# A conv-attention hybrid on one core: order of score copies, moved squares and the k projection in layer 1

## The chip, the core and the metric

The kernel runs on one core of a Trainium2 chip. The metric is the device time of one execution in microseconds (us); the time before is the median of three runs. Layer 1 of each of the eight images is the stage that the change touches. All arithmetic is fp32.

## What is computed

The input is x of shape (8, 256, 32, 32): eight images, each seen as 1024 tokens of 256 channels.

Layer 0 projects tokens to q, k and v for 8 heads of width 64, softens the scores over the *query* axis, applies them to v, projects with w_out and adds the input. Layer 1 is:

```python
t = _to_tokens(x)
t = t + _L1_attn_ref(_ln_t(t), L1_attn_W)
t = t + _L1_ffn_ref(_ln_t(t), router_w, w1, b1, w2, b2)
# _L1_attn_ref(n, W):
xa = einsum('bnd,ed->bne', n, W)
scores = einsum('bne,bme->bnm', xa, n)
y = einsum('bnm,bmd->bnd', softmax(scores, axis=-1), n)
```

So layer 1's attention has one head of width 256 whose keys and values are both the normed tokens n. The last line is a mixture of eight experts of which each token uses two.

## The kernel before, in words

**Stages.** Images are taken one after another. For image b, `layer0` runs the eight heads in pairs; then `attend` runs layer 1's attention; then `normed` and `logits` prepare the routing. For the first seven images the expert work is put off: rows are sent out in the next image's layer 0, and one routed pass (`experts`) handles them after the last image's layer 0. The last image uses `dense`. While layer 1 of image b runs, three kinds of work of image b+1 that do not depend on it are offered as filler by class `Begin`: its projection to q (t = 0), its projection to k (t = 1), each four matmuls of 128x512 in two accumulations (`project`, L349) with two evictions by ScalarE (L336), and its values (`values`, L408), two matmuls for each block of 128 tokens and an add by VectorE (L416). `Begin.at(place)` is called at "norm 1", "normed 1", "last weights", "last products", "norm 2" and "normed 2"; each call makes one block of values, and "norm 1" makes q and "norm 2" makes k. The remaining two blocks come from `rest` in the next layer 0.

**attend.** `layer_norm` makes n1, `to_channels` turns it (nT), and WT times nT gives px for two halves of the channels (L700). One level of a seven-product (Strassen-Winograd) scheme computes the scores: the 1024x1024 score matrix is seen as 2x2 halves. xa is kept as a11, a12, a22, s3_ and the mixes t1_ to t4_, s1_, s2_, s4_ (L689 to L716). ScalarE copies a22 and then a12 out of PSUM (L712, L713); VectorE then makes s1_ from a22 (L714), s2_ (L715) and s4_ (L716).

Rows are handled in four pairs, `Pair(k)` for k = 0 to 3: block k of the upper half and block k of the lower half, 128 rows each. The constructor makes five of the seven products (L750): a11·b11 into x, which ScalarE copies to the left half of the even block's buffer (L738, called `one_` before and `self.first` after); a12·b21 into v; s2_·t2_ on top of x, copied to the right half (L742, `self.second`); s1_·t1_ into z; s3_·t3_ on top of x, copied to the odd block's right half (L745). VectorE adds v and z to two of the halves and keeps their minima (L760). `rest` adds the last two products (s4_·b22 into z, a22·t4_ on top of x). It then takes the maxima and softens: the even block by L760 and one activation over 1024 (L781); the odd block by L784 and two activations of 512, one out of PSUM (L788) and one in SBUF (L796). x and v are the two banks of one tile of a pool of three ("big"), which px, the projections, the transposes and the values also use. z is in a pool of two that the mixings use too.

**Turning.** The mixing y = P·n needs the softened block with keys on partitions. For the first and the last block of BLOCKS, `turn_now` transposes by TensorE (L832) and VectorE copies the result out (L834). For the six blocks between, `turn` lets VectorE transpose squares of 32x32 in place (L814) and then moves sixteen strips of squares, 32x256 each: eight by ScalarE copies, eight by DMAs of SyncE (both recorded as L825). `issue_after(ins)` around a move makes it follow `ins` on the engine of `ins`; on other engines it adds nothing.

**Mixing.** `mix(at, ...)` does eight matmuls of 128x256 (L842; in the trace sixteen records) and divides by the sum and adds the residual (L851). The order in the code is: pairs 0 and 1, rest of 0, the second block turned, rest of 1, the third block turned, `turn_now(0)`, pair 2, the fourth block turned, mixings 0 to 2, and so on; `mix(7)` is last.

**What sets the order.** [...] In the trace this is not the order of the code: where an instruction that is traced earlier is not expected to be ready, one traced later is put before it. So the k projection, traced after the last mixing, runs between mixings. After the last mixing VectorE takes statistics (L256, L257), ScalarE the square root (L260), VectorE scales (L261, L263), TensorE transposes n2 (L281) and VectorE copies it (L282); then come the logits (L895) and the next image's first scores (L489).

Of the kernel before, what the change touches and what calls it, by code (L numbers as in the profile page):

```python
# [12 lines left out]
AF = mybir.ActivationFunctionType  # L13
ALU = mybir.AluOpType
# [5 lines left out]
def kernel(  # L20
# [23 lines left out]
    nc = tc.nc  # L44
# [18 lines left out]
    NQ = P // SQ  # L63
# [25 lines left out]
    def big(name):  # L89

        return ps_big.tile([P, 1024], F32, tag="big", name=name)
# [6 lines left out]
    scrap = const.tile([P, 512], F32, name="scrap")  # L98
# [231 lines left out]
    evicted = {}  # L330
# [54 lines left out]
    class Begin:  # L385
# [35 lines left out]

        def at(self, place):

            if place == "norm 1" or place == "norm 2":
                self.project(True)
            self.values(1)

        def all(self):
# [241 lines left out]
    def attend(b, t1, fill, tick=nothing):  # L670
# [13 lines left out]
        HALF = S // 2  # L684
# [8 lines left out]
        a11, s3_, a12, a22 = (xa[:, e, n, :] for e in range(2) for n in range(2))  # L693
        s1_, s2_, s4_ = (mixes[:, 4 + i, :] for i in range(3))
        pxs = []
        for ec in range(NCC):
            px = big(f"px_{b}_{ec}")
            for dc in range(NCC):
                for n in range(NH2):
                    nc.tensor.matmul(  # L700
                        px[:, ts(n, 512)],
                        WT[:, dc, ts(ec, P)],
                        nT[:, dc, ts(n, 512)],
                        start=(dc == 0),
                        stop=(dc == NCC - 1),
                    )
            pxs.append(px)
            if ec == 0:
                nc.scalar.copy(a11, px[:, :HALF])
                tick(("xa", ec), nc.vector.tensor_sub(s3_, a11, px[:, HALF:]))  # L710
            else:
                nc.scalar.copy(a22, px[:, HALF:])  # L712
                nc.scalar.copy(a12, px[:, :HALF])  # L713
                nc.vector.tensor_add(s1_, a22, pxs[0][:, HALF:])  # L714
                nc.vector.tensor_sub(s2_, s1_, a11)  # L715
                tick(("xa", ec), nc.vector.tensor_sub(s4_, a12, s2_))  # L716
# [5 lines left out]
        class Pair:  # L722

            def __init__(self, k):
                self.k = k
                both = big(f"ps1_{b}_{k}")
                self.x, v = both[:, :HALF], both[:, HALF:]
                self.z = acc(f"ps1z_{b}_{k}")
                self.ex = [homes[EX[2 * k + h]] for h in range(2)]
                self.low = [  # L730
                    small.tile([P, 1], F32, tag=f"nlow{h}", name=f"nlow_{b}_{k}_{h}")
                    for h in range(2)
                ]
                left, right = (self.ex[0][:, ts(n, HALF)] for n in range(2))
                far = self.ex[1][:, ts(1, HALF)]
                at = ts(k, P)
                self.product(self.x, a11, b11, True)
                one_ = nc.scalar.copy(left, self.x)  # L738
                second = self.product(v, a12, b21, True)
                tc.declare_no_dep(second.ins, one_.ins, reason="the other bank")  # L740
                self.product(self.x, s2_, t2_, False)
                self.second = nc.scalar.copy(right, self.x)  # L742
                self.product(self.z, s1_, t1_, True)
                self.product(self.x, s3_, t3_, False)
                nc.scalar.copy(far, self.x)  # L745
                self.add(left, v, 3.0e38, self.low[0])
                self.add(far, self.z, 3.0e38, self.low[1])
# [23 lines left out]
            def rest(self):  # L771
                k = self.k
                self.product(self.z, s4_, b22, False)
                self.product(self.x, a22, t4_, False)
                nmax, ssum = [], []
                for h in range(2):
                    nmax.append(small.tile([P, 1], F32, tag="nmax", name=f"nmax_{b}_{2 * k + h}"))
                    ssum.append(small.tile([P, 2], F32, tag="ssum", name=f"ssum_{b}_{2 * k + h}"))
                ex0, ex1 = self.ex
                tick(("max", 2 * k), self.add(ex0[:, HALF:], self.z, self.low[0], nmax[0]))  # L780
                nc.scalar.activation(  # L781
                    ex0, ex0, AF.Exp, bias=nmax[0], scale=-1.0, accum_out=ssum[0][:, 0:1]
                )
                last = nc.vector.tensor_scalar(  # L784
                    scrap, self.x, -1.0, self.low[1], ALU.mult, ALU.min, accum_out=nmax[1]
                )
                tick(("max", 2 * k + 1), last)
                nc.scalar.activation(  # L788
                    ex1[:, :HALF],
                    self.x,  # L790
                    AF.Exp,
                    bias=nmax[1],
                    scale=1.0,
                    accum_out=ssum[1][:, 0:1],
                )
                nc.scalar.activation(  # L796
                    ex1[:, HALF:],
                    ex1[:, HALF:],
                    AF.Exp,
                    bias=nmax[1],  # L800
                    scale=-1.0,
                    accum_out=ssum[1][:, 1:2],
                )
                return [(2 * k, ex0, ssum[0][:, 0:1], None), (2 * k + 1, ex1, *self.halves(ssum[1]))]

            def halves(self, ssum):
                return ssum[:, 0:1], ssum[:, 1:2]

        def turn(i, ex, behind):


            at_sq, at_aT = SQ_AT[i]
            sq = homes[at_sq]
            nc.vector.transpose(sq, ex)  # L814
            if at_aT is None:
                aT = two.tile([P, S], F32, tag="tr", name=f"aT_{b}_{i}")
            else:
                aT = homes[at_aT]
            to = aT.rearrange("p (m a q) -> p a m q", a=NQ, q=SQ)
            since = sq.rearrange("p (m k q) -> p k m q", k=NQ, q=SQ)  # L820
            for a in range(NQ):
                for k in range(NQ):
                    move = nc.sync.dma_start if (a + k) % 2 else nc.scalar.copy
                    with tc.issue_after(behind.ins) if behind else nullcontext():
                        move(to[ts(k, SQ), a], since[ts(a, SQ), k])  # L825
            return [aT[:, ts(m, P)] for m in range(NT)]

# [9 lines left out]
        def mix(at, aT, ssum, more):  # L837
            i = BLOCKS[at]
            ahead = fill("last products") if at == NT - 1 else None
            py = acc(f"py_{b}_{i}")  # L840
            for m in range(NT):
                nc.tensor.matmul(  # L842
                    py[:, :D], aT[m], n1[:, m, :], start=(m == 0), stop=(m == NT - 1)
                )
            rs = small.tile([P, 1], F32, tag="rs1", name=f"rs1_{b}_{i}")
            if more is not None:
                nc.vector.tensor_add(rs, ssum, more)
                ssum = rs
            nc.vector.reciprocal(rs, ssum)
            with tc.issue_after(ahead.ins) if ahead else nullcontext():  # L850
                mixed = nc.vector.scalar_tensor_tensor(  # L851
                    t2[:, i, :], py[:, :D], rs, t1[:, i, :], ALU.mult, ALU.add
                )
            tick(("mixed", at), mixed)
# [3 lines left out]
        def turned(at, ex, ssum, more, behind=None):  # L858
            return at, turn(at, ex, behind), ssum, more

        pairs = [Pair(0), Pair(1)]
        first, second = pairs[0].rest()
        second = turned(*second)
        third, fourth = pairs[1].rest()
        third = turned(*third)
        now = turn_now(0, first[1])
        pairs.append(Pair(2))
        fourth = turned(*fourth, pairs[2].second)
        mix(0, now, *first[2:])
        mix(*second)  # L870
        fifth, sixth = pairs[2].rest()
        fifth = turned(*fifth)
        mix(*third)
        pairs.append(Pair(3))
        sixth = turned(*sixth, pairs[3].second)
        mix(*fourth)
        seventh, eighth = pairs[3].rest()
        seventh = turned(*seventh)
# [432 lines left out]
    class Results:  # L1311
# [96 lines left out]
        def tick(self, place, behind=None):  # L1408
            added, sent, stored = self.PLACES.get(place, (0, 0, 0))
            if place == ("max", 0):  # L1410
                self.scored = behind
            if added:
                with tc.issue_after(behind.ins):
                    for _ in range(added):
                        self.add()
            for _ in range(sent):
                self.gather(behind)
            for _ in range(stored):
                if self.whole:
                    b, total, n = self.whole.pop(0)  # L1420
                    store(b, total, n)
# [135 lines left out]
    for b in range(B):  # L1557
# [16 lines left out]
        norm = None  # L1574
# [54 lines left out]
```

## Time and profile before

| what | value |
|---|---|
| median of 3 runs | 2346.41 us (2345.22 to 2347.16) |
| the profiled execution, own time | 2352.09 us |
| its span, first to last instruction | 2350.1 us |
| granted TensorE clock, mean | 0.992 |
| TensorE busy | 2270.4 us, 97% of the span |
| VectorE, ScalarE, GpSimd busy | 1560.2, 1165.0, 412.1 us |
| moves of squares by ScalarE (L825), three groups | 102.9 + 25.7 + 25.6 us for 384 copies |
| one image's TensorE work in layer 1, 902.8 to 994.2 us | 89.33 us busy of 91.40 |
| start to start from one image to the next, images 1 to 5 | 242.8 us |

In a timeline each row gives the start and the duration in us, the engine, the line, the operation with output and inputs, and how many instructions were merged. The bracket has the idle time of the engine just ahead of the row, and the instruction that ended it. "SPq" is SyncE's queue of DMA issues; its durations are those of issuing, not of the data. A busy TensorE can be one whose matmul ends are modelled.

### The profile page before, as it was taken

Reading aid. Unit: us, or ns where it says so; the run is one execution under the profiler, and the core shown is the slowest. Engines: PE = TensorE matmul, PEld = TensorE weight load, DVE = VectorE, ACT = ScalarE, POOL = GpSimd, SP = SyncE. Lnnn points to the kernel's source line nnn. Section 1 sums busy time; section 2 is a strip of 40 time slices with the busy share of each in tenths; the row PEclk is TensorE's granted clock in tenths of the full one; section 3 lists DMA queues with packets and bytes.
Section 4 is the critical chain, followed back from the end, with each engine's and each line's share of the span. In section 5 each row is a group of like instructions: output and inputs, shape, how many; then the busy total and the mean of one; then the engine's idle time right before and its main releaser. Section 6 shows DMA issues by size and latency. Waiting matters only on the chain.

```text
span 2350.1 us, 37998 instructions
## 1 busy us (share of the span) xinstructions
PE 2270.4 (97%) x13059; PEld 1213.5 (52%) x13059; DVE 1560.2 (66%) x4029; ACT 1165.0 (50%) x2139; POOL 412.1 (18%) x392
## 2 busy tenths in 40 slices
PE   9999999999999999999999999999999899999798
PEld 3345534553456335633564355435553278885465
DVE  5775578557865786578647775677568856435765
ACT  3664466446635663656464646465546522224321
POOL 0000012000200030003000200020002125444663
PEclk9999999999999999999999999999999999999899
DMA  8995201020103010201020101100110237665664
GB/s 295 385 386 141 68 15 42 7 57 10 46 1 57 12 51 1 45 19 50 5 46 19 46 10 27 37 23 15 21 43 19 71 99 196 182 188 152 189 196 136
DMA packets 278760, 200.10 MB, mean 85 GB/s; under 512 B 189576, under 2 KB 232232, under 8 KB 276776
## 3 DMA queue, kind: packets, MB, share of 16 engines
q1 hardware_dynamic: 252472, 139.14, 21.0%
q0 software_dynamic: 25008, 58.01, 7.7%
q8 instruction: 104, 1.70, 0.3%
q10 hardware_dynamic: 1088, 0.52, 0.1%
q14 instruction: 88, 0.72, 0.1%
HBM read 108.88 MB, written 110.90 MB: 94 GB/s over the span
## 4 chain that ended last, share of the span: by engine, by line
PE 82%; ACT 5%; DVE 5%; DMA 4%; issue 3%; SPq 0%; POOL 0%; DVEq 0%; ACTq 0%; POOLq 0%
PE po L566 18%; PE psc L489 18%; PE py L842 7%; PE pqk L371 7%; PE pr L663 5%; PE ps L750 4%; PE pv L408 4%; PE ph L1246 3%; PE pe L1272 3%; PE pdh L1495 2%; PE px L700 2%; PE pdy L1519 2%; PE pqk L349 2%; PE ps1z L750 1%; DMA y<-yb 1%
## 5 line engine op out<-in xcount | busy, mean ns | idle before, releaser
L530 ACT ACTIVATE ex<-psc,nmax 128x1024 f32<-128x1024 f32 x512 | 570.5, 1115 | 308.8 <-DVE scrap L513 225.3
L489 PE MATMUL psc<-qk,qk 64*64 64x512 f32 x4096 | 580.3, 593 | 3.6 <-ACT ex L530 3.5
L566 PE MATMUL po<-ex,vs 64*64 64x512 f32 x4096 | 570.9, 593 | 10.3 <-SPq L576 9.4
L513 DVE TENSOR_SCALAR_CACHE_REDUCE scrap<-psc,nmax 128x512 f32<-128x512 f32 x512 | 384.4, 751 | 165.6 <-PE psc L489 137.9
L504 DVE TENSOR_REDUCE nmax<-psc 128x1 f32<-128x512 f32 x512 | 350.6, 685 | 10.8 <-PE psc L489 10.8
L489 PEld LDWEIGHTS psc<-qk,qk 64*64 64x64 f32 x4096 | 180.6, 132 | 282.2 <-ACT ex L530 130.2
L566 PEld LDWEIGHTS po<-ex,vs 64*64 64x64 f32 x4096 | 175.0, 132 | 285.3 <-issue 83.9
L1060 POOL DMA_INDIRECT rows<-n,d_at x112 | 109.2, 975 | 656.8 <-DVE nmax L504 656.5
L987 POOL TENSOR_TENSOR t<-t,n 128x2048 f32<-128x2048 f32 x8 | 36.2, 4524 | 900.9 <-DVE n L263 744.2
L371 PE MATMUL pqk<-xT,wqkv 128*128 128x512 f32 x384 | 171.2, 599 | 0.1
L336 ACT ACTIVATE qk<-pqk,b_qks 128x512 f32<-128x512 f32 x124 | 85.6, 690 | 122.3 <-PE pqk L371 77.2
L408 PE MATMUL pv<-wqkv,xT 128*128 128x512 f32 x256 | 123.5, 604 | 1.5 <-DVE v L416 1.0
L842 PE MATMUL py<-n,spare 128*128 128x256 f32 x512 | 117.3, 383 | 5.8 <-DMA out_dram<-oT 3.8
L1368 POOL DMA_INDIRECT yk<-y,yat x112 | 112.0, 1000 | 61.6 <-issue 24.7
L371 PEld LDWEIGHTS pqk<-xT,wqkv 128*128 128x128 f32 x384 | 71.0, 190 | 100.0 <-issue 76.5
L842 PEld LDWEIGHTS py<-n,spare 128*128 128x128 f32 x512 | 98.2, 192 | 32.7 <-issue 20.0
L663 PE MATMUL pr<-wo,res 128*128 128x256 f32 x512 | 111.9, 379 | 0.0
L663 PEld LDWEIGHTS pr<-wo,res 128*128 128x128 f32 x512 | 97.2, 190 | 17.0 <-ACT res L585 3.2
L825 ACT COPY spare<-home 32x256 f32<-32x256 f32 x256 | 102.9, 402 | 3.2
L1256 ACT ACTIVATE hb<-ph,wb 128x256 f32<-128x256 f32 x96 | 40.4, 471 | 125.7 <-issue 86.6
L530 ACT ACTIVATION_READ_ACCUMULATOR ex<-psc,nmax 128x1 f32 x512 | 99.0, 193 | 0.0
L1246 PE MATMUL ph<-xb,wb 128*128 128x256 f32 x384 | 91.8, 381 | 6.3 <-DMA wb<-wpack,w_at 4.7
(256 smaller groups left out, 2895.9 us busy)
## 6 DMA issues: line engine op xcount, KB each, us to landing
rows<-wb SPq DMA_DIRECT2D x7, 8192.0 KB
xr<-rows SPq DMA_DIRECT2D x252, 64.0 KB
y<-yb POOLq DMA_DIRECT2D x63, 256.0 KB
xs<-in_x_dram SPq DMA_DIRECT2D x64, 128.0 KB
spare<-home SPq DMA_DIRECT2D x256, 32.0 KB
out_dram<-oT SPq DMA_DIRECT2D x60, 128.0 KB
xT<-in_x_dram SPq DMA_DIRECT2D x7, 1024.0 KB
sums<-t SPq DMA_DIRECT2D x7, 1024.0 KB
```

The source lines that it names most:

```text
L371: mm = nc.tensor.matmul(pq[:, ts(n, 512)], wqkv[:, cc, t, ts(g, P)], xT[:, cc, ts(n, 512)], start=(cc == 0), stop=(cc == NCC - 1),)
L408: nc.tensor.matmul(pv, self.xT[:, cc, ts(i, P)], wqkv[:, cc, 2, :], start=(cc == 0), stop=(cc == NCC - 1),)
L489: mm = nc.tensor.matmul(pss[at, h][ts(c, DK), ts(n, 512)], k[r, j * P + c * DK : j * P + (c + 1) * DK], q[r, ts(n, 512)], start=True, stop ...
L504: firsts[at, h] = nc.vector.tensor_reduce(nmax, pss[at, h][:, ts(0, 512)], AX.X, ALU.max, negate=True)
L513: seconds[h] = nc.vector.tensor_scalar(scrap, pss[at, h][:, ts(1, 512)], -1.0, nmaxes[at, h], ALU.mult, ALU.min, accum_out=nmax,)
L530: nc.scalar.activation(ex, pss.pop((at, h)), AF.Exp, bias=nmaxes.pop((at, h)), scale=1.0, accum_out=sums[at][:, h : h + 1],)
L566: mm = nc.tensor.matmul(po[n][ts(h, DK), :], vss[at][keys, h, :], exps[at, h][keys, ts(n, 512)], start=(j == 0 and turn == 0), stop=(j == ...
L663: nc.tensor.matmul(pr[:, :C], res[:, g, ts(i, P)], wo[:, g, :], start=(g == 0), stop=(g == NPAIR - 1))
L750: return nc.tensor.matmul(to, stationary[:, ts(self.k, P)], moving, start=start, stop=True, skip_group_check=not start,)
L842: nc.tensor.matmul(py[:, :D], aT[m], n1[:, m, :], start=(m == 0), stop=(m == NT - 1))
L1246: last = nc.tensor.matmul(ph[:, ts(fc, BR)], wb[:, dc * FF + fc * P : dc * FF + (fc + 1) * P], xb[:, dc, :], start=(dc == 0), stop=(dc == ...
L1368: ins = nc.gpsimd.indirect_dma_start(out=self.slot(at)[:, k, :], out_offset=None, in_=self.group.y[:, :], in_offset=bass.IndirectOffsetOnAxis(
```

## The change

Four edits, all in layer 1's attention or in its fillers:

1. a12 is copied ahead of a22.
2. In pair 1 the odd block is softened ahead of the even one, so that the activation which reads the pair's PSUM comes first. Other pairs keep the order.
3. `turn` takes a pair of instructions to stay behind: the first for strips a = 0 and 1, the second for a = 2 and 3. The third block's turn moves in the code behind `turn_now(0)` and `Pair(2)`; its ScalarE moves are held behind pair 2's first copy (L738) for half of the strips and its second (L742) for the others. The fourth and sixth blocks stay behind the second copy of the next pair, as before.
4. The k projection ("norm 2") is issued on TensorE behind the last matmul of the last mixing.

```diff
@@ Begin.at
-            if place == "norm 1" or place == "norm 2":
+            if place == "norm 1":
                 self.project(True)
+            elif place == "norm 2":
+                with tc.issue_after(evicted["mixed"].ins):
+                    self.project(True)
             self.values(1)
@@ attend
             else:
+                nc.scalar.copy(a12, px[:, :HALF])
                 nc.scalar.copy(a22, px[:, HALF:])
-                nc.scalar.copy(a12, px[:, :HALF])
@@ Pair.__init__
-                one_ = nc.scalar.copy(left, self.x)
+                self.first = nc.scalar.copy(left, self.x)
                 second = self.product(v, a12, b21, True)
-                tc.declare_no_dep(second.ins, one_.ins, reason="the other bank")
+                tc.declare_no_dep(second.ins, self.first.ins, reason="the other bank")
@@ Pair.rest
+                def even():
+                    tick(("max", 2 * k), self.add(ex0[:, HALF:], self.z, self.low[0], nmax[0]))
...
+                def odd():
+                    last = nc.vector.tensor_scalar(
+                        scrap, self.x, -1.0, self.low[1], ALU.mult, ALU.min, accum_out=nmax[1]
+                    )
...
+                for half in (odd, even) if k == 1 else (even, odd):
+                    half()
@@ turn
-        def turn(i, ex, behind):
+        def turn(i, ex, behind=None):
...
-                    with tc.issue_after(behind.ins) if behind else nullcontext():
+                    with tc.issue_after(behind[a * 2 // NQ].ins) if behind else nullcontext():
                         move(to[ts(k, SQ), a], since[ts(a, SQ), k])
@@ mix
-                nc.tensor.matmul(
+                evicted["mixed"] = nc.tensor.matmul(
                     py[:, :D], aT[m], n1[:, m, :], start=(m == 0), stop=(m == NT - 1)
                 )
@@ attend, the order
         third, fourth = pairs[1].rest()
-        third = turned(*third)
         now = turn_now(0, first[1])
         pairs.append(Pair(2))
-        fourth = turned(*fourth, pairs[2].second)
+        third = turned(*third, (pairs[2].first, pairs[2].second))
+        fourth = turned(*fourth, (pairs[2].second, pairs[2].second))
         mix(0, now, *first[2:])
...
-        sixth = turned(*sixth, pairs[3].second)
+        sixth = turned(*sixth, (pairs[3].second, pairs[3].second))
```

More of the change, by code (lines that the diff above doesn't have):

```diff
@@ L779, in rest @@
                 ex0, ex1 = self.ex
[L780 to L803, printed above, removed]
+                def even():
+                    tick(("max", 2 * k), self.add(ex0[:, HALF:], self.z, self.low[0], nmax[0]))
+                    nc.scalar.activation(
+                        ex0, ex0, AF.Exp, bias=nmax[0], scale=-1.0, accum_out=ssum[0][:, 0:1]
+                    )
+                def odd():
+                    last = nc.vector.tensor_scalar(
+                        scrap, self.x, -1.0, self.low[1], ALU.mult, ALU.min, accum_out=nmax[1]
+                    )
+                    tick(("max", 2 * k + 1), last)
+                    nc.scalar.activation(
+                        ex1[:, :HALF],
+                        self.x,
+                        AF.Exp,
+                        bias=nmax[1],
+                        scale=1.0,
+                        accum_out=ssum[1][:, 0:1],
+                    )
+                    nc.scalar.activation(
+                        ex1[:, HALF:],
+                        ex1[:, HALF:],
+                        AF.Exp,
+                        bias=nmax[1],
+                        scale=-1.0,
+                        accum_out=ssum[1][:, 1:2],
+                    )
+                for half in (odd, even) if k == 1 else (even, odd):
+                    half()
                 return [(2 * k, ex0, ssum[0][:, 0:1], None), (2 * k + 1, ex1, *self.halves(ssum[1]))]
```

## The prediction, made before the change was run

> **What bounds the kernel now.** I read the page first, then the timeline of TensorE, ScalarE and SyncE over one image's layer 1. Part 1 of the page says that TensorE is the bound:
>
> ```profile
> PE 2270.4 (97%) x13059; PEld 1213.5 (52%) x13059; DVE 1560.2 (66%) x4029; ACT 1165.0 (50%) x2139; POOL 412.1 (18%) x392
> ```
>
> A change of order leaves TensorE's work as it is, so it can only win the stalls between matmuls. Image 3 stands for images 1 to 6, which repeat to about 0.1 us (the stage's TensorE busy time is 89.2 to 89.4 us in each). TensorE's timeline there (start, duration, instruction, and in brackets the idle time and who ended it):
>
> ```profile
> 930.64 1.02 PE L750 MATMUL ps<-nT,xa 128*128 128x512 f32 x2
> 931.96 1.12 PE L750 MATMUL ps<-nT,xa 128*128 128x512 f32 x2 [0.30 <-ACT xa L713]
> ...
> 945.13 1.88 PE L750 MATMUL ps<-nT,xa 128*128 128x512 f32 x4
> 947.25 1.98 PE L750 MATMUL ps<-nT,xa 128*128 128x512 f32 x4 [0.25 <-ACT home L788]
> 949.12 3.72 PE L842 MATMUL py<-n,aT 128*128 128x256 f32 x16
> 952.68 1.02 PE L408 MATMUL pv<-wqkv,xT 128*128 128x512 f32 x2
> 955.06 1.98 PE L750 MATMUL ps<-mixes 128*128 128x512 f32 x4 [1.36 <-ACT home L738]
> ...
> 981.10 3.62 PE L842 MATMUL py<-n,spare 128*128 128x256 f32 x16
> 984.55 2.74 PE L349 MATMUL pqk<-xT,wqkv 128*128 128x512 f32 x6
> 987.12 3.62 PE L842 MATMUL py<-n,spare 128*128 128x256 f32 x16
> 990.58 3.62 PE L842 MATMUL py<-n,aT 128*128 128x256 f32 x16
> 994.03 1.88 PE L408 MATMUL pv<-wqkv,xT 128*128 128x512 f32 x4
> 997.25 0.44 PE L281 MATMUL pt_n<-ident,n 128*128 128x128 f32 x2 [1.34 <-DVE n L263]
> ```
>
> Back to back, two records of a 512-wide product start 0.86 us apart (940.82 and 942.54 hold four, 1.72), so the true stalls, start against expected start, are a little longer than the brackets: 931.96 - 931.50 = 0.46; 947.25 - 946.85 = 0.40; 955.06 - 953.54 = 1.52; 997.25 - 995.75 = 1.50, and 0.29 more ahead of the logits at 1001.16. Sum **4.2 us an image**. The causes are in ScalarE's timeline:
>
> ```profile
> 946.43 0.67 ACT L788 ACTIVATE home<-ps,nmax 128x512 f32<-128x512 f32 x1
> 947.10 3.28 ACT L825 COPY aT<-home 32x256 f32<-32x256 f32 x8
> 950.39 0.72 ACT L796 ACTIVATE home<-home,nmax 128x512 f32<-128x512 f32 x1
> 951.11 3.28 ACT L825 COPY spare<-home 32x256 f32<-32x256 f32 x8
> 954.42 1.07 ACT L738 COPY home<-ps 128x512 f32<-128x512 f32 x2
> ```
>
> Pair 2's first score copy (L738) had its product ready near 946 and runs at 954.42, behind sixteen moves of squares. The other half of the moves goes through SyncE, which issues one after another at 0.65 us:
>
> ```profile
> 952.05 10.44 SPq L825 DMA_DIRECT2D spare<-home  x16
> 965.67 5.96 SPq L825 DMA_DIRECT2D home<-home  x8
> 971.74 10.44 SPq L825 DMA_DIRECT2D spare<-home  x16
> ```
>
> The last eight of these are the seventh turn's. They are issued by 982.18, and its mixing starts at 987.12 after the six k-projection records at 984.55.
>
> [...] this trace's chain of waits has the same for a SyncE move, 2.00 us at 227.65 in image 0, which I use. [...] the trace has 1283 ns at L260[...].
>
> **The change, part by part (one of images 1 to 6).**
>
> *a12 copied before a22.* The second product needs a12 only, so its 0.46 us wait goes. But a22 is then 0.48 later (931.32 for 930.84), so L714, which makes s1_, starts at 931.95 and ends at 932.64, and the next product, free at 932.36, waits some 0.35 for it. Gain 0.1 (0 to 0.46).
>
> *Odd half of pair 1 softened first.* Same three activations and two maxima, other order. L788, which frees the pair's two PSUM banks, goes from 946.43 to about 945.30; pair 3's products no longer wait: 0.40. Next late would be the first mixing at 949.12, which waits for the copy of pa (L834, 947.88 to 949.07) behind two transposes of 1.25; the copy is now traced ahead of the second of these, so it can run near 946.7. The third block's exponential ends at about 947.9 instead of 946.4; SyncE is busy with the second block's moves until 951.88, which hides it. Gain 0.4 (0 to 0.6).
>
> *Moves of the third block held.* Nothing is added: sixteen moves stay, eight by ScalarE at 0.41, eight DMAs by SyncE; the hold orders only ScalarE's, as the instruction waited for is ScalarE's. ScalarE needs from 945.30 2.5 us for pair 1 and 3.3 for the second block's moves, so L738 can run at 951.15 instead of 954.42. TensorE's first mixing ends at 952.1 to 952.6: the 1.52 us wait is gone. What is queued behind: four moves of the third block wait for L738, four for L742 (a product of 0.9 later), then the fourth block's eight, to about 959.5 if nothing stalls. The third mixing needs the DMAs, issued by 957.1, landed at 959.1; it would start near 959.8, so they are covered by 0.7. Pair 3's first copy, which today runs beside pair 2's, now loses to all these moves: near 959.5 in a gap, or behind pair 2's exponentials and the fifth block's moves near 966.3. In the second case TensorE lacks work ahead of the fourth mixing (landed at 964.5, free near 963.3: 1.2) and around the seventh. I take 0.9 given back of 1.5: gain 0.6 (-2.0 to 1.5).
>
> *k projection behind the last mixing.* Eight records, 3.44 us, and two evictions at 0.69 move behind 993.9. There VectorE's chain from the last mixing to pt_n takes 3.1 us; the projection covers all of it, and the values' add of 0.69 that today sits ahead of the reciprocal (995.95) can go. So the 1.79 us of the tail is covered. The loss is in front: the six records at 984.55 bridged the seventh turn's transfers. Those land at 982.18 + 2.0 = 984.2; without the 0.86 of projection at 980.24 the sixth mixing ends at 983.7: 0.5 bare, and where the remaining pv products fill it, they are missing in the tail. The evictions' readers, the next image's scores, come 6 us later: hidden. 0.7 is given back: gain 1.1 (-1.0 to 1.8, the low end being the third rival).
>
> Sum per image: 0.1 + 0.4 + 0.6 + 1.1 = **2.2**; images 1 to 6: **13.2**. Image 0 has the same stalls but waits of its own for transfers (1.3 more at 225.82): **1.6**. Image 7 has no projection to move; its stall at 2169.06 is 2.22, but its sixth and seventh mixings wait 3.79 and 1.98 for moves that SyncE issues between loads and stores held by VectorE, and those need not come sooner: **0.5** (-3 to 3). In all 15.3 us. The profiled execution took 2352.1 (span 2350.1), so it would take 2336.8; the median of runs is 2346.4, which gives **2331**.
>
> **Rivals.** *The last pair comes late* (slower). Pair 3's copies wait in ScalarE's queue; if its exponentials come later, the seventh turn's DMAs do, and nothing is left to bridge. Start of the seventh mixing plus 6.9 for two mixings plus 6.7 for the tail's chain against today's 1001.16 gives break-even at 987.55, moves landed 3.4 us later than today's 984.2. If the copies fall behind one more block of moves (3.3) and a product with its wait (1.3), it is 4.6: 1.2 lost an image, 8.4 in seven, **2355**. For it: pair 3 is traced last. Against: today there are 19 us from its first copy to its exponential (974.32), while pair 2 needs 8.7.
>
> *The fillers are spent early* (no change). With the projection barred, the pv products fill the waits ahead of the sixth and seventh mixings, and the tail is again bound by its chain, bare for 1.4 of today's 1.8; with the held moves' gain given back whole, 0.5 an image remains: **2343**.
>
> *The eviction gets ahead of the square root* (half the gain). The first k eviction is ready about 1.9 us after the last mixing, the root (L260) about 1.8. In the wrong order the root waits 0.69, and the table load, today done early at 988.03, may fall between: 1.28 more. About half of these 2 us is covered by other products: 1.0 lost an image, **2338**.
>
> That the edit does nothing is excluded for the k projection, which can no longer run at 984.55.
>
> **How the numbers follow.** Forecast 0.58 (its own range 2322 to 2340), late pair 0.14, fillers 0.16, eviction 0.12. About 0.2% (4.7 us) is what a measurement of this kernel can tell from no change. Faster: 0.57 + 0.09 + 0.02 = 0.68; the same: 0.01 + 0.03 + 0.12 + 0.03 = 0.19; slower: 0.02 + 0.11 = 0.13. If every stall went, 4.2 x 7 + 3 would give 2314; the low end, 2319, stops short of it, and the high end, 2349, reaches over the no-change case to the nearer edge of the late pair.
>
> **What would show it.** Right: no stall at the second product over 0.35; L788 of pair 1 ahead of L781; L738 of pair 2 near 951; eight L349 records in a row behind the last mixing; pt_n's wait gone. Wrong: a stall ahead of the seventh mixing over 1 us, pair 3's L738 behind the fifth block's moves, or L336 ahead of L260. If these outweigh the 4.2 us, the sign is wrong.

## The result, and the profile after

The changed kernel takes **2327.56 us** (median of six runs, 2326.5 to 2330.9), the kernel before 2346.78 us on the same chip (six runs, 2345.22 to 2351.31). The ratio is 0.9917, 95% interval [0.9904, 0.9929]: faster by 0.8%. The forecast was 2331.

The profiled execution took 2327.18 us with a span of 2325.2, so the span fell by 24.9 where the medians fell by 19.2; the profiled execution of before was itself 5.3 above its median. Cut at the starts of the eight px (the product that opens layer 1's attention in each image), it divides like this:

| stretch | before | after | difference | forecast |
|---|---|---|---|---|
| to px of image 0 | 189.43 | 189.51 | +0.1 | 0 |
| px of image 0 to px of image 1 | 248.71 | 247.87 | -0.8 | -1.6 |
| images 1 to 5, sum | 1214.59 | 1200.73 | -13.9 | -11.0 |
| image 6 | 483.25 | 475.11 | -8.1 | -2.2 |
| image 7, to the end | 214.12 | 211.98 | -2.1 | -0.5 |

Image 6's stretch contains the last layer 0 and the routed experts. Up to the transposition of the logits (plT) it won 2.45 like the others (84.93 to 82.48 after px); the other 5.7 lie in work that the change does not touch, about the 5.3 by which that execution of before was high. That part of image 6 lasts 390.6 to 398.3 us in the fourteen traces, and before has the longest; so the 5.7 are read as scatter of that one execution, a reading that no run was made for. Without them 19.2 are left, for 15.3 forecast.

The first line of the page: TensorE is still the bound, with the same number of matmuls.

```profile
PE 2259.1 (97%) x13059; PEld 1211.7 (52%) x13059; DVE 1561.8 (67%) x4029; ACT 1167.0 (50%) x2139; POOL 411.2 (18%) x392
```

TensorE's timeline over image 3 (start, duration, instruction, idle time and who ended it). In the changed kernel the lines have moved: L750 is L753, L738 and L742 are L741 and L745, L781, L788 and L796 are L786, L795 and L803, L825 is L835, L842 is L852, L895 is L905.

```profile
924.45 2.82 PE L753 MATMUL ps<-nT,xa 128*128 128x512 f32 x6
...
941.89 2.75 PE L852 MATMUL py<-n,aT 128*128 128x256 f32 x12
945.11 1.13 PE L753 MATMUL ps<-mixes 128*128 128x512 f32 x2 [0.47 <-ACT home L741]
946.07 1.03 PE L852 MATMUL py<-n,aT 128*128 128x256 f32 x4
947.38 1.12 PE L753 MATMUL ps<-mixes,xa 128*128 128x512 f32 x2 [0.28 <-ACT home L745]
...
959.54 1.02 PE L753 MATMUL ps1z<-mixes 128*128 128x512 f32 x2
961.89 1.12 PE L753 MATMUL ps<-mixes,xa 128*128 128x512 f32 x2 [1.33 <-ACT home L745]
...
974.07 7.38 PE L852 MATMUL py<-n,spare 128*128 128x256 f32 x32
981.29 3.62 PE L852 MATMUL py<-n,aT 128*128 128x256 f32 x16
984.74 3.60 PE L349 MATMUL pqk<-xT,wqkv 128*128 128x512 f32 x8
...
989.89 1.91 PE L281 MATMUL pt_n<-ident,n 128*128 128x128 f32 x16
...
993.45 1.07 PE L905 MATMUL pl<-n2T,rT 128*32 128x256 f32 x16
994.45 1.93 PE L492 MATMUL psc<-qk,qk 64*64 64x512 f32 x12
```

The waits at the second product (924.45 has six records without one), at pair 3's first products and of the tail are gone, and the sixth and seventh mixings stand in one row (974.07). That row hides a small wait: its 32 records take 7.22 us by starts, where 32 of 0.216 (sixteen took 3.45 before, 974.19 to 977.64) would take 6.91, and the 0.3 lie ahead of the seventh mixing, at 977.76. And the middle did not become free: three waits for score copies stand there, by starts 0.64 + 0.45 + 1.49 = **2.58 us**. Before there were 0.46 + 0.40 + 1.52 = 2.38 in front of the tail. So all of the win is in the tail, and in the middle the three other edits have cancelled one another.

The tail of before held more than the prediction counted. Its logits (pl) and the next image's first scores (psc) ran like this, and the second half of the logits' input was copied until 1002.24 (VectorE's row):

```profile
1001.16 0.64 PE L895 MATMUL pl<-n2T,rT 128*32 128x256 f32 x8
1001.73 1.07 PE L489 MATMUL psc<-qk,qk 64*64 64x512 f32 x2
1002.73 0.64 PE L895 MATMUL pl<-n2T,rT 128*32 128x256 f32 x8
1003.30 1.93 PE L489 MATMUL psc<-qk,qk 64*64 64x512 f32 x10
1005.16 3.70 PE L408 MATMUL pv<-wqkv,xT 128*128 128x512 f32 x8
```

```profile
999.88 2.36 DVE L282 COPY n2T<-pt_n 128x1024 f32<-128x1024 f32 x2 [0.43 <-PE pt_n L281]
```

From the first logits to the next values the same 28 matmuls took 4.00 us before (1001.16 to 1005.16) and take 2.87 after (993.45 to 996.32): 1.13 more, and no bracket shows it. It is a cost of the order and not idle time: two scores stand between the halves of the logits, and they take 1.00 us by starts, while the other ten take 1.86 and all twelve together take 1.87 after (0.99 of the 1.13); the logits in two rows take 1.14 for 1.00 in one. The tail was 1.50 + 0.29 + 1.13 = **2.92**, the whole image 5.30, and 5.30 - 2.58 = 2.72 is about what an image of 2.67 less shows in image 3 (2.77, 242.92 to 240.15, in the mean of images 1 to 5).

Why the middle didn't win is in ScalarE's timeline:

```profile
938.63 0.67 ACT L795 ACTIVATE home<-ps,nmax 128x512 f32<-128x512 f32 x1
...
940.04 3.30 ACT L835 COPY aT<-home 32x256 f32<-32x256 f32 x8
943.35 1.15 ACT L786 ACTIVATE home<-home,nmax 128x1024 f32<-128x1024 f32 x1
...
944.49 0.56 ACT L741 COPY home<-ps 128x512 f32<-128x512 f32 x1
...
953.80 0.59 ACT L741 COPY home<-ps 128x512 f32<-128x512 f32 x1
...
961.25 0.59 ACT L745 COPY home<-ps 128x512 f32<-128x512 f32 x1
```

Pair 1's odd half is softened first (L795), as the edit says. But the second block's eight moves are then put between the halves (940.04), so the even exponential, and with it the third block's turn, comes after them (943.35). Pair 2's first copy runs at 944.49, 26.9 after px. Pair 3's runs at 953.80, 36.2 after px (31.1 before), and its second at 961.25, behind the fifth block's moves; TensorE waits 1.49 for it.

### The profile page after: what moved, and what is told of

It reads as the page before. It is cut to its first block, busy times and chain, and to the rows that moved or that the text cites. A ratio compares the mean times of both kernels' runs of the same rounds, so it can differ in the third digit from the quotient of the medians.

```text
span 2325.2 us, 37960 instructions
## 1 busy us (share of the span) xinstructions
PE 2259.1 (97%) x13059; PEld 1211.7 (52%) x13059; DVE 1561.8 (67%) x4029; ACT 1167.0 (50%) x2139; POOL 411.2 (18%) x392
## 4 chain that ended last, share of the span: by engine, by line
PE 80%; ACT 6%; DVE 5%; DMA 4%; issue 3%; SPq 1%; POOL 0%; DVEq 0%; ACTq 0%; POOLq 0%
PE po L569 19%; PE psc L492 18%; PE pqk L371 7%; PE py L852 6%; PE pr L666 5%; PE pv L408 4%; PE ps L753 3%; PE ph L1256 3%; PE pe L1282 3%; PE pdy L1529 2%; PE pdh L1505 2%; PE px L703 2%; PE pqk L349 2%; DMA y<-yb 1%; ACT aT L835 1%
## 5 line engine op out<-in xcount | busy, mean ns | idle before, releaser
L492 PE MATMUL psc<-qk,qk 64*64 64x512 f32 x4096 | 573.0, 593 | 3.6 <-ACT ex L533 3.5
L336 ACT ACTIVATE qk<-pqk,b_qks 128x512 f32<-128x512 f32 x124 | 85.6, 690 | 86.6 <-PE pqk L371 77.5
L852 PE MATMUL py<-n,spare 128*128 128x256 f32 x512 | 118.0, 386 | 3.9 <-DMA out_dram<-oT 3.2
L852 PEld LDWEIGHTS py<-n,spare 128*128 128x128 f32 x512 | 98.3, 193 | 29.0 <-issue 16.4
L835 ACT COPY spare<-home 32x256 f32<-32x256 f32 x256 | 103.0, 402 | 10.1 <-DVE home L824 6.7
```

What stands on the lines that cost most here:

```text
L492: mm = nc.tensor.matmul(pss[at, h][ts(c, DK), ts(n, 512)], k[r, j * P + c * DK : j * P + (c + 1) * DK], q[r, ts(n, 512)], start=True, stop ...
L852: evicted["mixed"] = nc.tensor.matmul(py[:, :D], aT[m], n1[:, m, :], start=(m == 0), stop=(m == NT - 1))
```

## The experiments

A to D are edits 1 to 4 in the order of the list above. The kernels differ in the order of work alone. Totals of kernels that ran on different chips are compared as ratios to the kernel before on the same chip (its medians were 2346.8 to 2365.5). The stretch from one px to the next is sharper: the changed kernel has the same mean to 0.01 us in two runs. The table has it as a mean of images 1 to 5, then for image 3 alone beside the waits found there by start against expected start, from px to the logits; the 1.13 of the tail counts as one of them. (For the run of the values it is image 2.)

| kernel | ratio, 95% | images 1 to 5 | image 3 | waits | rest |
|---|---|---|---|---|---|
| before | 1 | 242.92 | 242.84 | 5.30 | 237.5 |
| changed | 0.9917 [0.9904, 0.9929] | 240.15 | 240.17 | 2.58 | 237.6 |
| D alone | 0.9911 [0.9894, 0.9927] | 240.16 | 240.54 | 3.02 | 237.5 |
| A, B, D | 0.9957 [0.9942, 0.9972] | 240.90 | 240.90 | 3.33 | 237.6 |
| C alone | 0.9969 [0.9961, 0.9978] | 242.19 | 242.07 | 4.51 | 237.6 |
| changed, fifth held | 0.9920 [0.9904, 0.9936] | 239.65 | 239.61 | 1.98 | 237.6 |
| B alone | 1.0057 [1.0044, 1.0070] | 244.26 | 244.19 | 6.71 | 237.5 |
| A alone | 0.9976 [0.9968, 0.9983] | 242.47 | 242.36 | 4.85 | 237.5 |
| A, C, D | 0.9878 [0.9862, 0.9894] | 238.85 | 238.87 | 1.25 | 237.6 |
| values behind | 0.9964 [0.9951, 0.9977] | 242.16 | 241.08 | 3.54 | 237.5 |
| changed, even ahead | 0.9922 [0.9909, 0.9936] | 239.82 | 240.07 | 2.23 | 237.8 |
| A, C, D, fifth held | 0.9856 [0.9844, 0.9869] | 238.80 | 238.80 | - | - |
| changed, again | 0.9908 [0.9893, 0.9924] | 240.15 | - | - | - |
| even ahead, second | 0.9911 [0.9893, 0.9929] | 239.31 | 239.34 | 1.80 | 237.5 |

The last column carries the accounting: an image is 237.5 to 237.8 us plus its waits, in every order counted. Not in the list are the 0.3 us hidden ahead of the seventh mixing, which five kernels have: the changed one, the rows "A, B, D" and "A, C, D", and the two with the even half ahead; with them the rest is 237.3 to 237.6. Alone, the edits are worth -0.45 (A), +1.34 (B), -0.73 (C) and -2.76 (D); their sum is -2.60, and together they gave -2.77. They add up in the combinations too: 241.05 and 238.98 by these sums for "A, B, D" and "A, C, D", measured 240.90 and 238.85.

### D alone

```diff
+            elif place == "norm 2":
+                with tc.issue_after(evicted["mixed"].ins):
+                    self.project(True)
...
-                nc.tensor.matmul(
+                evicted["mixed"] = nc.tensor.matmul(
```

> The kernel before with the fourth edit alone (k projection behind the last mixing). Theory from the two traces: the stretch from the last mixing to the next image's token transposes of the logits is 2.98 us an image shorter after the change, and the stretch ahead of it 0.32 longer; if that is all this edit's doing, 2.66 x 7 = 18.6 us are won, ratio 0.992, as much as by the whole change. Rival (the sum on record): 1.1 an image, 7.7 us, ratio 0.9967.

2343.13 us, ratio 0.9911: this one edit gives the steady images all that the whole change gives them. From px to the end of the last mixing image 3 needs 67.7 us for 70.4; from there to plT it needs 14.94 for 14.51. The projection's 3.44 us left the front, and the tail took them for 0.43.

```profile
973.53 3.69 PE L845 MATMUL py<-n,spare 128*128 128x256 f32 x16 [0.47 <-issue]
...
980.51 3.60 PE L349 MATMUL pqk<-xT,wqkv 128*128 128x512 f32 x8
```

### A, B and D: the holds undone

```diff
         third, fourth = pairs[1].rest()
+        third = turned(*third)
         now = turn_now(0, first[1])
         pairs.append(Pair(2))
-        third = turned(*third, (pairs[2].first, pairs[2].second))
```

> The changed kernel with the third block's turn where it was before and not held; the other three edits stay. Theory: between the first mixing and the copy of the last block the change lost 1.06 us an image (a stall of 1.49 ahead of pair 3's third product, 0.63 and 0.45 ahead of pair 2's), so without the hold the kernel is some 7 us faster than the changed one: about 2320, ratio to before 0.9885. Rival (the sum on record): the hold wins 0.6 an image, so 2327.6 + 4.8 = 2332, ratio 0.994.

2353.59 us, and 240.90 an image: without the holds it is 0.75 *slower*. The theory read from the two traces alone, that the holds cost what B had won, falls. ScalarE's timeline of this kernel shows what they do: unheld, the third block's eight moves run in one piece ahead of pair 2's second copy.

```profile
950.06 3.30 ACT L835 COPY spare<-home 32x256 f32<-32x256 f32 x8 [0.84 <-DVE home L824]
953.38 0.59 ACT L745 COPY home<-ps 128x512 f32<-128x512 f32 x1
```

In the changed kernel two moves are there (0.82), and the wait for this copy is 0.45 instead of 1.20.

### C alone

(on the kernel before; `turn` takes the pair of instructions as in the change)

```diff
-        third = turned(*third)
         now = turn_now(0, first[1])
         pairs.append(Pair(2))
-        fourth = turned(*fourth, pairs[2].second)
+        third = turned(*third, (pairs[2].first, pairs[2].second))
+        fourth = turned(*fourth, (pairs[2].second, pairs[2].second))
```

> The kernel before with the third edit alone (third block's turn later in the code and held behind pair 2's copies). Theory: slower by 1.06 us in each of eight images, 8 us, ratio 1.0036. Rival (the sum on record): faster by 0.6 x 7 = 4 us, ratio 0.998. Third case: the hold needs the odd block softened first, and alone it does something else again.

2358.95 us, 0.9969: faster by 0.73 an image, against the theory and close to the 0.6 on record. The 1.52 before pair 2's products became 0.34 + 0.38 by starts, at pair 2's two copies; for pair 3's copies nothing is waited for, and the 0.40 for the pair's PSUM stays.

```profile
949.22 1.12 PE L750 MATMUL ps<-mixes 128*128 128x512 f32 x2 [0.18 <-ACT home L738]
...
951.86 1.12 PE L750 MATMUL ps<-mixes,xa 128*128 128x512 f32 x2 [0.22 <-ACT home L742]
```

### The changed kernel with the fifth block held too

```diff
-        fifth = turned(*fifth)
+        pairs.append(Pair(3))
+        fifth = turned(*fifth, (pairs[3].first, pairs[3].second))
         mix(*third)
-        pairs.append(Pair(3))
```

> The changed kernel with pair 3 made ahead of the fifth block's turn in the code and the fifth block's ScalarE moves held behind pair 3's copies, as the third block's are behind pair 2's. If the stall of 1.49 us ahead of pair 3's third product is there because pair 3's second copy runs behind the fifth block's eight moves, it goes: up to 1.3 us an image, 9 us, 2318. Rival: the fifth block's moves come 1.2 to 2.4 us later, its mixing waits for them instead, and the time stays at 2327 or is some us longer.

2345.02 us, 0.9920. The wait of 1.49 for pair 3's second copy is gone, as meant, but 0.5 an image is won instead of 1.3: a 0.40 for VectorE's minima and a 0.50 at the last transposes stand there instead.

### B alone

```diff
-                for half in (even, odd):
+                for half in (odd, even) if k == 1 else (even, odd):
```

> The kernel before with the second edit alone (odd block of pair 1 softened first). Theory: this edit is the one that loses. In the changed kernel pair 1's even exponential runs behind the second block's eight moves, so the third block is transposed 4 us later and pair 2's and pair 3's copies with it; the steady images lose about 1.2 us each (0.8 lost by the first two edits together, and 0.4 won by the first), and image 0 about 6: slower by 13 us, ratio 1.0055. Rival (the sum on record): 0.4 an image faster, ratio 0.9985.

2372.40 us, 1.0057: B makes the kernel slower, as expected here. It removes the wait it was meant for (0.40) and brings 0.64, 1.20 and 1.49 for the 1.52 that was there, each for a score copy.

```profile
961.83 1.12 PE L750 MATMUL ps<-mixes 128*128 128x512 f32 x2 [0.47 <-ACT home L738]
...
966.57 1.13 PE L750 MATMUL ps<-mixes,xa 128*128 128x512 f32 x2 [1.04 <-ACT home L742]
...
979.37 1.12 PE L750 MATMUL ps<-mixes,xa 128*128 128x512 f32 x2 [1.33 <-ACT home L742]
```

In image 0 it costs 7.4 us (256.08 for 248.71).

### A alone

```diff
+                nc.scalar.copy(a12, px[:, :HALF])
                 nc.scalar.copy(a22, px[:, HALF:])
-                nc.scalar.copy(a12, px[:, :HALF])
```

> The kernel before with the first edit alone (a12 copied ahead of a22). Theory: in the changed kernel pair 1's first product was put into the gap that the later a22 leaves, so the whole wait of 0.46 us goes: 0.46 x 8 = 3.7 us, ratio 0.9984. Rival (the sum on record): 0.1 an image, no change. Third case: as the loss of 0.8 an image belongs to the first two edits together, it could be this one's: ratio above 1.002.

2353.38 us, 0.9976, 0.45 an image: the whole wait at the second product, with nothing in its place. TensorE's timeline shows why s1_, though later, is not waited for: six records stand where two did, so another product of data that was ready lies before the one that reads s1_ (L750, ps1z).

```profile
929.04 2.82 PE L750 MATMUL ps<-nT,xa 128*128 128x512 f32 x6
931.70 1.02 PE L750 MATMUL ps1z<-mixes 128*128 128x512 f32 x2
```

### A, C and D: pair 1 even first again

```diff
-                for half in (odd, even) if k == 1 else (even, odd):
+                for half in (even, odd):
```

> The changed kernel without the second edit (even block first in every pair). If the odd half first is what loses, this is the fastest so far: steady images 242.8 - 0.46 - 0.75 - 2.75 = 238.9 us against 240.1 of the changed kernel, image 0 some 5 us shorter: 12 us ahead of the changed kernel, ratio to before 0.987. Rival: pair 3's products again wait for the pair's PSUM (0.40 an image), and the rest is as in the changed kernel: ratio 0.993.

2329.89 us, 0.9878: taking B back wins 1.30 an image and 5.9 in image 0. ScalarE's timeline (px at 909.18): the second block's moves come after both PSUM readers, and pair 3's first copy (938.16) directly behind four moves of the third block, 29.0 after px.

```profile
931.35 0.67 ACT L795 ACTIVATE home<-ps,nmax 128x512 f32<-128x512 f32 x1
...
932.02 3.28 ACT L835 COPY aT<-home 32x256 f32<-32x256 f32 x8
...
936.03 0.56 ACT L741 COPY home<-ps 128x512 f32<-128x512 f32 x1
936.50 1.64 ACT L835 COPY spare<-home 32x256 f32<-32x256 f32 x4
938.16 0.58 ACT L741 COPY home<-ps 128x512 f32<-128x512 f32 x1
```

### Values, in place of the k projection, behind the last mixing

```diff
+            if place == "last weights" or place == "last products":
+                return
+            if place == "norm 2":
+                with tc.issue_after(evicted["mixed"].ins):
+                    for _ in range(3):
+                        self.values(1)
+                return
             self.values(1)
```

(on the kernel before; the k projection stays free to run early)

> The kernel before with the k projection left free, and two other blocks of values (together 3.44 us of TensorE work, as much as the projection) kept for behind the last mixing in its place. If what wins is the amount of work that is left for the tail, it wins as much as the k projection there: 2.7 us an image, ratio 0.991. Rival: it is the order on ScalarE and VectorE, since values end in adds of 0.69 us on VectorE, which carries the tail's chain, while the projection's evictions go to ScalarE: the chain waits for up to three such adds and half of the gain or more is lost, ratio 0.995 or above.

2350.01 us, 0.9964, less than D. The tail is covered all the same (15.06 us from the last mixing to plT, with 12 records of values ahead of the transposes), so VectorE's adds of the values do not delay its chain. What was lost lies in front: pair 2's wait, which two records of values filled in part, is bare, 2.48 for 1.52. In images 3 to 5 the same wait cost more than itself. TensorE's timeline of image 3:

```profile
948.69 3.11 PE L757 MATMUL ps<-mixes 128*128 128x512 f32 x4 [2.21 <-ACT home L745]
951.59 1.64 PE L757 MATMUL ps<-mixes,xa 128*128 128x512 f32 x2
```

Four records take 2.90 us by starts for 1.72, with the granted clock at 0.50 from 949.40 on (the last part has the windows). These images are 242.7 to 243.1 us, images 1 and 2 are 241.1.

### The changed kernel, the second block's moves behind the even exponential

```diff
-                    nc.scalar.activation(
+                    self.softened = nc.scalar.activation(
...
-        second = turned(*second)
         third, fourth = pairs[1].rest()
+        second = turned(*second, (pairs[1].softened, pairs[1].softened))
```

(`softened` is the even half's activation)

> The changed kernel with all four edits, and with the second block's ScalarE moves held behind pair 1's even exponential, so that softening the odd block first no longer puts eight moves (3.3 us) ahead of it. If that is how the second edit loses, its loss of 1.3 us in a steady image and 7 in image 0 is gone: steady images at 238.9 us or up to 0.4 less (pair 3's wait for PSUM goes too), ratio 0.987 or less, as the kernel without the second edit (0.9878). Rival: the odd block's early copies themselves, or the later moves of the second block, cost it: steady images stay near 240.1, ratio 0.9915.

2330.58 us, 0.9922. With the eight moves out of the way an image gains 0.33 of the 1.30, not most of it: the theory that they are the whole cause falls. Pair 3's first copy still comes 35.4 after px.

### A, C and D with the fifth block held

The edit of the fifth block on A, C and D.

> The kernel without the second edit (ratio 0.9878) with pair 3 made ahead of the fifth block's turn and the fifth block's moves held behind pair 3's copies. Without the second edit pair 3's second copy already runs ahead of the fifth block's moves, so there is nothing left to win there: within 0.2% of 0.9878. Rival: as with all four edits, 0.5 us a steady image more (there 240.1 became 239.65): ratio 0.986.

2314.36 us, 0.9856, the fastest of all. In images 1 to 5 the hold brings 0.05; where pair 3's second copy isn't late there is nothing to win. The rest came from images 6 and 7 (1.5 and 9.4 in the profiled executions); see the end of the next part.

### The changed kernel once more

> The changed kernel itself, on the same chip as the two above. Ratio 0.9917 as measured before, steady images 240.1 us.

2325.47 us, 0.9908, and 240.15 an image: the same to 0.01.

### Even ahead, and the third block wholly behind pair 2's second copy

```diff
-        third = turned(*third, (pairs[2].first, pairs[2].second))
+        third = turned(*third, (pairs[2].second, pairs[2].second))
```

(on the kernel with the even exponential ahead)

> The changed kernel with the second block's moves held behind pair 1's even exponential (as in the run even-ahead), and with all eight ScalarE moves of the third block held behind pair 2's second copy instead of four behind the first and four behind the second. That leaves ScalarE a gap between pair 2's two copies, in which pair 3's first copy could run if the planner lets it. Theory, that the odd-first order costs its remaining 0.9 us an image because pair 3's first copy comes late (35.4 us after px where it is 29.1 with the even half first): if the copy moves to about 31 us or earlier, the steady images fall from 239.8 to about 239.0 us and the run to about 0.9885 of before. Rival, that pair 2's copies and its stalls of 1.3 to 1.7 us ahead of pair 3's products are the cost by themselves (TensorE earlier, ScalarE not): the images stay at 239.6 to 240.0 wherever pair 3's copy goes, ratio 0.992. If the copy doesn't move, the run tells nothing between the two.

2337.86 us, 0.9911. Pair 3's first copy moved, to 27.3 after px, directly behind pair 2's (the two copies at 937.85; px at 911.00):

```profile
937.85 1.07 ACT L741 COPY home<-ps 128x512 f32<-128x512 f32 x2
```

The images fell from 239.82 to 239.31, half way to the theory's 239.0 and below the rival's 239.6. What is left is one wait of 1.47 by starts, for pair 2's first copy:

```profile
935.30 1.89 PE L852 MATMUL py<-n,aT 128*128 128x256 f32 x8
938.49 1.12 PE L753 MATMUL ps<-mixes 128*128 128x512 f32 x2 [1.29 <-ACT home L741]
```

## Why the prediction was right, step by step

**The total held, with two of its steps wrong by nearly the same amount**: B was 1.7 us an image too hopeful, D 1.7 too cautious. That the total came so close is luck to that extent.

*a12 ahead (0.1 forecast, 0.45 measured).* The wait at the second product went, as said. The step that failed is the 0.35 that the next product would wait for s1_: it assumed that the products keep their order, and the compiler's planner put a ready one in between.

*Odd half first (gain 0.4 forecast, loss 1.34 measured).* L788, now L795, did run early and its wait went. The step that failed is "Same three activations and two maxima, other order", with the second block's moves left where they were. ScalarE works with hardly a pause from pair 0's exponentials to pair 2's first copy (in image 3 of the changed kernel it is busy for 8.28 of the 8.38 us from 936.11 to 944.49); the copy comes 26.9 us after px in the changed kernel, in A, C and D, and in both kernels with the even half ahead. A TensorE that is earlier waits for it the longer; the 0.40 had to come back. On top of that the new order made other work late. The runs divide the 1.30 between A, C and D and the whole change into three: 0.33 for the second block's moves between the halves, 0.51 for the late pair 3 (the run that moved its first copy forward; it moved the third block's moves too), and 0.46 left over, where the longer wait at pair 2's first copy stands (1.47 with the even half ahead and the later hold, 0.45 in A, C and D, which has the 0.40 besides). Why the planner puts pair 3's copies so late once the odd half is first was not isolated.

*Holds (0.6 forecast, 0.73 alone, 0.75 with the others).* Right in size. The wait that came back is at pair 2's copies, not at pair 3's as the step had it. In the changed kernel pair 3's second copy did run behind the fifth block's moves, but as B's doing: B alone has the same wait of 1.49, C alone has none.

*k projection (1.1 forecast, 2.76 measured).* The mechanism was right: eight L349 records behind the last mixing, no waits in the tail. Two terms were mis-sized. "So the 1.79 us of the tail is covered": the tail was 2.92. The prediction corrected the rows that had a bracket, and put at nothing the 1.13 that the split logits and the scores between them cost, where no row has one. "0.7 is given back": 0.25 was. D alone reaches the end of the last mixing 3.19 us earlier in the mean of images 1 to 5, with 3.44 less work in front; image 3 is the worst of them with 2.73, and 0.63 bare ahead of the seventh mixing. SyncE's last moves in the changed kernel are issued by 975.9, 58.3 after px, as before (982.18, 58.4 after px):

```profile
963.24 12.65 SPq L835 DMA_DIRECT2D spare<-home  x16
```

The seventh mixing starts at 977.76, 60.2 after px and 1.87 behind the end of the last issue. That is close to the 2.00 from a move's issue to its use in the trace of before (227.65, image 0), so its wait of 0.3 is read as one for these moves, of the kind that the prediction put at 0.5.

*Rivals.* "The last pair comes late" did not happen: the seventh mixing starts 60.2 after px, where it was 63.4 before. "The fillers are spent early" did not: eight records of values stand in the tail. "The eviction gets ahead" did not; the square root (L260) runs at 986.35, the first eviction (L336) behind it at 986.66.

*Image 0 (1.6 forecast, 0.8 measured, 2.1 in the second run).* D alone wins 5.1 there and B alone loses 7.4. TensorE's clock has a part in these: in image 0 it stood at 0.50 for 3.41 us before, 6.83 in the changed kernel, 3.41 in its second run and 13.65 with B alone, and for none with D alone or with A, C and D. *Image 7 (0.5 forecast, 2.1 measured)*: the wait of 2.22 at pair 2's copy went, the two before the sixth and seventh mixing are 3.19 and 0.34 for 3.79 and 1.98.

**What stays open** is image 7 in the variants. From px to the end it is 212.0 and 212.2 us in the two runs of the changed kernel and 214.1 before, but 215.6 to 232.9 in the others: A, C and D has a wait of 7.69 us for VectorE at one mixing, the last run one of 9.24 for VectorE's minima. There the experts' work of other images shares VectorE and SyncE with the attention, and each order places it anew. That is a reading, not shown by an experiment. The lengths themselves are measured, and because of them the totals of the variants do not follow from their steady images, and D alone, with image 7 at 231.2, is no measure of what the other edits are worth in the total.

## What to carry to other kernels

List the waits by start against expected start for every row, with or without a bracket, and compare how long the same matmuls take before and after, since an order can cost time without an idle moment (1.13 us in the tail here); one image was 237.5 to 237.8 us plus that list in every order counted. Before freeing an engine earlier, ask whether the engine that feeds it next can come earlier: with ScalarE busy for 8.28 of 8.38 us, TensorE's 0.4 came back as a wait, and the reordering cost 1.3 more. Test the edits one by one even when the total agrees: here one of four was a loss, and without it the kernel is at 0.9878 instead of 0.9917 (238.85 us an image instead of 240.15).

## What the hardware showed

With the values moved, the wait of 2.48 us (bracket 2.21) was followed by half of TensorE's granted clock in one image and not in another: the clock stayed at 1.00 in image 2, where the wait ended at 707.60, and was 0.50 in image 3, where it ended at 948.69. The windows of that run (length, busy times of TensorE, its weight loads, VectorE, ScalarE and GpSimd, granted clock, DMA share, GB/s):

```profile
703.64:707.05 3.41, 1.75 (x9) 1.20 (x7) 2.54 (x6) 3.31 (x11) 0.00 (x0) 1.00 0.30 48
707.05:710.47 3.42, 2.87 (x7) 1.26 (x8) 0.00 (x0) 2.64 (x6) 0.00 (x0) 1.00 0.31 49
...
945.99:949.40 3.41, 1.20 (x5) 0.56 (x4) 1.42 (x6) 3.06 (x7) 0.00 (x0) 1.00 0.31 48
949.40:952.82 3.42, 3.42 (x5) 1.33 (x5) 0.00 (x0) 2.60 (x6) 0.00 (x0) 0.50 0.30 48
```

In this run drops of the clock begin at 222.36, 949.40, 1191.75 and 1434.09, which is 213, 71 and 71 times 3.4133 us apart. In the traces of before and of the changed kernel, too, all drops are whole multiples of it apart, to 0.004 us (269.62 and 1826.10 before: 456 times), and the shortest stretch at 0.50 is 3.41 us. The windows are steps of that length. In image 3 the whole wait falls into one step, idle for 0.65 of it, and the next step has half the clock; in image 2 the same wait is divided, 0.49 and 0.16. Counted so over the fourteen traces (steps at full clock between 190 and 2090 us, idle as the profile has it), 30 of 30 steps with 0.60 or more idle were followed by half the clock, 2 of 10 with 0.47 to 0.53, and 1 of 7707 with less; the traces of before and of the changed kernel have 4 of 4, 0 of 2 and 1 of 1098 of these. Why the clock drops was not shown beyond these counts. In image 0 of the changed kernel two waits fell into one step; the mixing after them took 5.49 us by starts for 3.45:

```profile
226.39 1.12 PE L753 MATMUL ps<-mixes 128*128 128x512 f32 x2 [2.09 <-ACT home L741]
229.50 2.08 PE L753 MATMUL ps<-mixes,xa 128*128 128x512 f32 x2 [1.98 <-ACT home L745]
231.36 5.65 PE L852 MATMUL py<-n,aT 128*128 128x256 f32 x16
```

```profile
225.23:228.64 3.41, 1.12 (x2) 0.30 (x2) 0.69 (x3) 3.34 (x8) 0.00 (x0) 1.00 0.32 49
228.64:235.47 6.83, 5.97 (x12) 4.13 (x13) 1.02 (x4) 1.39 (x4) 0.00 (x0) 0.50 0.04 7
```

With the values moved, the stretch from px to the end of the last mixing took 69.75 us in images 3 to 5 and 68.15 in images 1 and 2, so in images 3 to 5 the wait cost 1.6 us more than itself.
